# Interleaving small expert units with whole blocks: two units behind the last block, and the gate product ahead of the output product

## The chip, the cores and the metric

The kernel runs on one core of a Trainium2 chip. The metric is the time on the device of one execution, in microseconds (us), as the median of several executions. A core has a matrix engine (TensorE, PE in the profile, with its weight loads as PEld), VectorE (DVE), ScalarE (ACT), GpSimd (POOL, which here issues all gathers and scatters by index), SyncE (SP), and 16 DMA engines between device memory and the on-chip memories. Each engine works through its own list of instructions in the order in which the compiler put them; semaphores make an instruction wait for another engine or for a transfer.

## The reference

The reference is one transformer layer on x of shape 2 x 4096 x 512, all in float32: a layer norm with modulation, linear attention with 16 heads, a residual, a second layer norm, and a mixture of 8 experts of which each token takes 2. What matters here is the last part:

```python
gate_out = ragged_dot(sorted_xs, w_gate)              # per expert, 512 -> 2 x 512
activation = gelu(gate_out[:, 0, :]) * gate_out[:, 1, :]
expert_outputs = ragged_dot(activation, linear)       # per expert, 512 -> 512
out = einsum('blkd,blk->bld', out_by_token, combine_weights)
x = x + gb * out
```

There are 8192 tokens, so 16384 pairs of token and expert. How many fall on each expert is known only when the router has run.

## The kernel before, in words

The pairs of each expert are cut into units. A whole block has 512 tokens of one expert; there are always 25 of them (9 early, 16 late: `NEARLY`, `NLATE`). What is left over goes through small units of 128 tokens, of which 29 (`NSURE`) are always worked through and a few more behind a branch on the count.

**A whole block** (`block`, L1645) multiplies with seven products of half-size matrices in place of eight (`seven`, L1502): seven products for the first half of the gate weights, seven for the second, seven for the output weights, 21 in all. `gate_big` ends with gelu on ACT and with products and sums on DVE (L1611, L1612, L1620 to L1623) that make the left operands `aT` and `aS` of `linear_big`. The block is a generator: it yields between products, 22 times for one block (`STEPS`).

**A small unit** has four parts:

- `fetch_small` (L1675) gathers the gate weights of the unit's expert (`wgs`, 128 x 4096 float32, 2.1 MB, one buffer), the map of its tokens, and the token rows (`xg_s`).
- `turn_in` (L1685) transposes the rows on PE (`pxs`) and copies them with ACT.
- `gate_small` (L1696) first gathers the output weights (`wls`, 128 x 2048 float32, 1.05 MB, one buffer), then runs the two gate products (`pgs`, L1705) and makes the activation `ar` on ACT and DVE.
- `turn_out` (L1716) transposes `ar` (`pas`), and `linear_small` (L1726) runs the output product (`py`, L1731). `put` (L1461) scales the result on DVE (`y_s`, L1485) and adds it to the output rows with an indirect DMA (`out`, L1488). Each unit's additions wait for those of the unit before, since they may meet in the same row.

With one buffer each, the gather of the next `wgs` waits until the gate product that reads the old one is done on PE, and the gather of the next `wls` waits for the output product that reads the old one.

**The order of the work.** `smalls` (L1736) is a generator too, with two steps for each turn j: the first turns out unit j - 1 and turns in unit j, the second holds the products. One more turn than there are units empties the pipeline, so 29 units make 60 steps. `in_turn` (L1753) advances the blocks one step at a time and lets the small units follow in a fixed proportion; what has not been run when the count of block steps is reached runs after the loop:

```python
for n in range(1, count_one + 1):
    next(one, None)
    while done < count_other * n // count_one:
        next(other, None)
        done += 1
for g in (other, one):
    for _ in g:
        pass
```

So the order of the instructions on PE is nearly that of the program, with small differences where the compiler's scheduler places them. In the last stage of the kernel the 16 late blocks (352 steps) are mixed with the 29 small units (60 steps). Before the change the 60 steps are spread over the first 345 block steps, and the last 7 steps, the output products of the last block, run alone.

Of the kernel before, what the change touches and what calls it, by code (L numbers as in the profile page):

```python
# [33 lines left out]
NBIG = (NTOK * TOPK - E * (TB - 1) + TB - 1) // TB  # L34

NEARLY = (N * TOPK - E * (TB - 1) + TB - 1) // TB
NLATE = NBIG - NEARLY
# [8 lines left out]
NSURE = 29  # L46
# [7 lines left out]
def adaln_linear_attention_moe_kernel(  # L54
# [83 lines left out]
    def pool(stack, name, bufs=1, **kw):  # L138
        return stack.enter_context(
            tc.tile_pool(name=name, bufs=bufs, reuse_waits="tile", **kw)  # L140
        )
# [876 lines left out]
    count = {"cum": sm.tile([P, E], FP, tag="cum", name="cum")}  # L1018
# [401 lines left out]
    def gather(dst, src, ids):  # L1420
        return nc.gpsimd.indirect_dma_start(  # L1421
            out=dst, out_offset=None, in_=src, in_offset=IndirectOffsetOnAxis(ap=ids, axis=0)
        )

    def flat(t):
        return t.rearrange("p a k n -> p (a k n)")
# [8 lines left out]
    def fetch_map(ns, j, mrow, bufs):  # L1435

        mp = lists.tile([P, ns, 2], FP, tag=f"mp{ns}_{bufs}", name=f"mp_{ns}_{j}", bufs=bufs)
        got = gather(
            mp.rearrange("p t s -> p (t s)"),
            map_d.rearrange("(r t) s -> r (t s)", t=ns),  # L1440
            mrow,
        )
        for sent in scatters:
            manual_dep(got.ins, sent, "the map is whole")
        return mp
# [4 lines left out]
    def fetch_rows(where, ns, key, mp, bufs, src):  # L1450

        xg = []
        for t in range(ns):
            r = where.tile([P, C], FP, tag=f"xg{ns}", name=f"xg_{key}_{t}", bufs=bufs)
            gather(r, src, token(mp, t))
            xg.append(r)
        return xg
# [187 lines left out]
    def block(j):  # L1645

        more = j + 1 < NBIG

        soon = more and j + 1 != NEARLY
        if more:  # L1650
            fetch_big_rows(j + 1)
        yield from gate_big(j, 0)
        if more:
            fetch_gate(j + 1, 0)
        yield
        yield from gate_big(j, 1)
        if more:
            fetch_gate(j + 1, 1)
        if NEARLY <= j + 1 and j + 2 < NBIG:
            fetch_big_map(j + 2)  # L1660
        yield
        if soon:
            turn_big(j + 1)
        yield
        yield from linear_big(j)
        if more:
            fetch_lin(j + 1)
        if more and not soon:
            turn_big(j + 1)
        yield  # L1670
# [4 lines left out]
    def fetch_small(j):  # L1675
        wg = sw.tile([P, 2, 4, KH, QN], FP, tag="wgs", name=f"wgs_{j}", bufs=1)
        mrow, wrow = late["rows"]
        gather(wg.rearrange("p m q k n -> p (m q k n)"), wgate, wrow[:, j : j + 1])
        if (1, j) not in maps:
            maps[1, j] = fetch_map(1, j, mrow[:, j : j + 1], 4)  # L1680
        small[j] = [fetch_rows(sw, 1, f"s{j}", maps[1, j], 2, h2_d), wg]
        if j + 1 < NSURE:
            maps[1, j + 1] = fetch_map(1, j + 1, mrow[:, j + 1 : j + 2], 4)

    def turn_in(j):  # L1685
        xg = small[j].pop(0)[0]
        xT = sw.tile([P, KC, P], FP, tag="xTs", name=f"xTs_{j}", bufs=2)
        pt = psum["t"].tile([P, TB], FP, tag="tr", name=f"pxs_{j}")
        for k in range(KC):
            nc.tensor.transpose(  # L1690
                pt[:, k * P : (k + 1) * P], xg[:, k * P : (k + 1) * P], ident
            )
        nc.scalar.copy(xT.rearrange("p k n -> p (k n)"), pt)
        small[j].append(xT)

    def gate_small(j):  # L1696

        xT, wg = small[j].pop(), small[j].pop()
        wl = sw.tile([P, 4, KH, QN], FP, tag="wls", name=f"wls_{j}", bufs=1)
        gather(flat(wl), wlin, late["rows"][1][:, j : j + 1])  # L1700
        pg = []
        for half, quarters in enumerate(((0, 1), (3, 2))):
            p = psum["g"].tile([P, 2, QN], FP, tag="g", name=f"pgs_{j}_{half}")
            for k in range(KC):
                nc.tensor.matmul(  # L1705
                    p, xT[:, k, :], wg[:, :, quarters[k // KH], k % KH, :],
                    start=(k == 0), stop=(k == KC - 1),
                )
            pg.append(p.rearrange("p m n -> p (m n)"))
        ge = sw.tile([P, H], FP, tag="ges", name=f"ges_{j}", bufs=2)  # L1710
        nc.scalar.activation(ge, pg[0], AF.Gelu_apprx_tanh)
        ar = sw.tile([P, H], FP, tag="ar", name=f"ar_{j}", bufs=2)
        nc.vector.tensor_tensor(ar, pg[1], ge, ALU.mult)
        small[j] += [wl, ar]

    def turn_out(j):  # L1716

        ar = small[j].pop()
        pt = psum["t"].tile([P, TB], FP, tag="tr", name=f"pas_{j}")
        for hc in range(HC):  # L1720
            nc.tensor.transpose(pt[:, hc * P : (hc + 1) * P], ar[:, hc * P : (hc + 1) * P], ident)  # L1721
        aT = sw.tile([P, HC, P], FP, tag="aTs", name=f"aTs_{j}", bufs=2)
        nc.scalar.copy(aT.rearrange("p k n -> p (k n)"), pt)
        small[j].append(aT)

    def linear_small(j):  # L1726
        wl, aT = small.pop(j)
        p = psum["g"].tile([P, 2, QN], FP, tag="g", name=f"py_{j}")
        for hc in range(HC):
            q = (slice(0, 4, 3), slice(1, 3))[hc // KH]  # L1730
            nc.tensor.matmul(  # L1731
                p, aT[:, hc, :], wl[:, q, hc % KH, :], start=(hc == 0), stop=(hc == HC - 1)
            )
        put(f"s{j}", maps.pop((1, j)), [[p.rearrange("p h n -> p (h n)")]], False)

    def smalls(count):  # L1736


        for j in range(count + 1):
            if j:  # L1740
                turn_out(j - 1)
            if j < count:
                turn_in(j)
            yield
            if j:
                linear_small(j - 1)
            if j < count:
                gate_small(j)
                if j + 1 < count:
                    fetch_small(j + 1)  # L1750
            yield

    def in_turn(one, count_one, other, count_other):  # L1753

        done = 0
# [8 lines that stand above are left out]
# [35 lines left out]
    STEPS = 3 * 7 + 1  # L1799

    def blocks(j0, j1):
        for j in range(j0, j1):
            yield from block(j)
# [9 lines left out]
    for _ in block(NEARLY - 1):  # L1813
# [4 lines left out]
    psum.clear()  # L1818
    psum["t"] = pool(ctx, "ps_t3", 2, space=PSUM)
    psum["g"] = pool(ctx, "ps_g3", 6, space=PSUM)  # L1820
    in_turn(
        blocks(NEARLY, NBIG), STEPS * NLATE - STEPS // 3, smalls(NSURE), 2 * (NSURE + 1)
    )

    left = nc.values_load(late["left"], min_val=0, max_val=NSMALL)

# [62 lines left out]
```

## Time and profile before

| | us |
|---|---|
| median of 3 runs | 2370.75 |
| lowest, highest | 2366.18, 2374.37 |
| profiled execution, time | 2372.11 |
| profiled execution, span of the trace | 2370.4 |
| PE busy in the span | 2257.7 |
| last stage, where late blocks and small units are mixed | from about 1423 to the end |

The span is the time from the first to the last instruction in the trace; the execution's own time is 1.71 us longer. A line of a timeline gives the start, the busy time, the engine, the source line, the operation with the tiles that it writes and reads, and in brackets how long the engine had been idle before it and what ended that.

### The profile page before, as it was taken

What the parts mean: (1) busy time and instruction counts of PE and PEld (TensorE: products, weight loads), DVE (VectorE), ACT (ScalarE), POOL (GpSimd) and SP (SyncE); (2) the same over time, 40 slices, a digit from 0 to 9 for tenths busy, and PEclk for the clock granted to TensorE, in tenths of its full rate; (3) what the DMA queues carried; (4) which work ended last, traced back from release to release, by engine and by line L of the source; (5) the groups of instructions that cost most, each with busy time, mean ns of one, the idle gap of its engine ahead of it and who ended that gap; (6) DMA issues with size and microseconds to landing.
All of it is one profiled execution on the core that took longest, in us unless ns stands there. A gap on an engine that the chain in (4) does not pass through costs nothing. (4 is left out here: it accounts for less than half of the span.)

```text
span 2370.4 us, 26081 instructions
## 1 busy us (share of the span) xinstructions
PE 2257.7 (95%) x9456; PEld 1702.1 (72%) x9456; DVE 1523.0 (64%) x3251; ACT 535.0 (23%) x976; POOL 963.2 (41%) x840
## 2 busy tenths in 40 slices
PE   8999989999988999989998889999999999999997
PEld 4576657777766758878887767777777777777775
DVE  4866647786977756767876765555555555555554
ACT  1121212232323302333333411111111111111110
POOL 1266663003223242343535356444444444544432
PEclk9999999999999999999999989999999999999999
DMA  7688886444544444647684557777777777777774
GB/s 271 244 310 324 333 313 230 166 152 138 178 164 110 127 160 166 215 152 239 171 256 150 162 169 241 250 249 247 249 250 250 235 237 248 244 249 256 245 222 89
DMA packets 120189, 513.29 MB, mean 217 GB/s; under 512 B 19365, under 2 KB 22181, under 8 KB 84090
## 3 DMA queue, kind: packets, MB, share of 16 engines
q0 software_dynamic: 64704, 296.79, 40.1%
q1 hardware_dynamic: 41530, 164.45, 20.4%
q10 hardware_dynamic: 13824, 50.34, 5.5%
q8 instruction: 77, 1.26, 0.2%
q14 instruction: 54, 0.44, 0.1%
HBM read 378.97 MB, written 132.55 MB: 216 GB/s over the span
## 5 line engine op out<-in xcount | busy, mean ns | idle before, releaser
L1512 PE MATMUL p_g<-xT,wg 128*128 128x256 f32 x1600 | 373.0, 380 | 0.0
L1512 PEld LDWEIGHTS p_g<-xT,wg 128*128 128x128 f32 x1600 | 303.4, 191 | 45.7 <-issue 5.2
L1512 PE MATMUL p_g<-xS,wg 128*128 128x256 f32 x1200 | 286.6, 381 | 14.9 <-DVE quar_l L1520 7.6
L1512 PEld LDWEIGHTS p_g<-xS,wg 128*128 128x128 f32 x1200 | 227.4, 191 | 51.2 <-issue 8.1
L946 PE MATMUL po<-gm,qT 128*128 128x265 f32 (+1 forms) x1024 | 247.2, 391 | 4.6 <-issue 2.6
L795 PE MATMUL pa<-k,xh 128*128 128x512 f32 x512 | 234.2, 611 | 16.4 <-ACT k L774 16.3
L946 PEld LDWEIGHTS po<-gm,qT 128*128 128x128 f32 x1024 | 194.3, 194 | 40.2 <-issue 5.5
L1488 POOL DMA_INDIRECT out<-y_b,mp x100 | 162.7, 1627 | 129.2 <-DVE y_b L1485 101.2
L1153 POOL DMA_INDIRECT map_d<-pair,slot x128 | 133.5, 1043 | 176.0 <-DVE slot L1150 138.4
L1705 PE MATMUL pgs<-wgs,xTs 128*128 128x512 f32 x464 | 203.9, 592 | 0.0
L1512 PE MATMUL p_l<-wl,aT 128*128 128x256 f32 x800 | 193.7, 380 | 2.6 <-DVE part_l L1520 2.6
L795 PEld LDWEIGHTS pa<-k,xh 128*128 128x128 f32 x512 | 99.0, 196 | 134.4 <-issue 108.1
L617 POOL TENSOR_TENSOR wraw<-wraw 128x512 f32<-128x512 f32 x96 | 135.7, 1417 | 88.9 <-DMA wraw<-in_wgate 36.0
L1705 PEld LDWEIGHTS pgs<-wgs,xTs 128*128 128x128 f32 x464 | 88.2, 190 | 110.5 <-issue 109.5
L1512 PEld LDWEIGHTS p_l<-wl,aT 128*128 128x128 f32 x800 | 148.8, 191 | 23.6 <-DVE part_l L1520 3.0
L1512 PE MATMUL p_l<-wl,aS 128*128 128x256 f32 x600 | 144.0, 383 | 0.6 <-DVE aS L1622 0.6
L679 POOL TENSOR_TENSOR xs<-xT 128x512 f32<-128x512 f32 x16 | 21.3, 1330 | 292.1 <-DMA xT<-in_xturned 173.1
L1520 DVE TENSOR_TENSOR quar_g<-part_g,p_g 128x512 f32<-128x512 f32 x150 | 102.5, 684 | 51.1 <-PE p_g L1512 46.5
L1611 ACT ACTIVATE ge<-quar_g 128x512 f32<-128x512 f32 x100 | 63.0, 630 | 312.2 <-DVE quar_g L1520 300.9
L1512 PEld LDWEIGHTS p_l<-wl,aS 128*128 128x128 f32 x600 | 114.3, 192 | 17.9 <-issue 1.4
L1421 POOL DMA_INDIRECT xg_b<-h_d,mp x100 | 100.9, 1009 | 64.1 <-issue 32.5
L1520 DVE TENSOR_TENSOR part_g<-part_g,p_g 128x512 f32<-128x512 f32 x100 | 68.5, 686 | 83.8 <-PE p_g L1512 78.8
(343 smaller groups left out, 3734.7 us busy)
## 6 DMA issues: line engine op xcount, KB each, us to landing
xT<-in_xturned SPq DMA_DIRECT2D x16, 1024.0 KB
x<-in_x SPq DMA_DIRECT2D x16, 1024.0 KB
q_d<-q ACTq DMA_DIRECT2D x64, 256.0 KB
xb_d<-x SPq DMA_DIRECT2D x16, 1024.0 KB
qi<-q_d SPq DMA_DIRECT2D x64, 256.0 KB
wraw<-in_wgate SPq DMA_DIRECT2D x16, 1024.0 KB
wgsum_d<-wraw SPq DMA_DIRECT2D x16, 1024.0 KB
xb<-xb_d SPq DMA_DIRECT2D x16, 1024.0 KB
```

Of the source, the lines that this page charges most:

```text
L617: nc.gpsimd.tensor_tensor(to, one, two, op)
L679: nc.gpsimd.tensor_tensor(s7, x00, x10, ALU.subtract)
L795: nc.tensor.matmul(pa, xh[t][:, g * P : (g + 1) * P], ks[t], start=(t == 0), stop=(t == NT - 1),)
L946: nc.tensor.matmul(po[:, C // 2 - EX + c0 : C // 2 - EX + c1], qT[:, g * P : (g + 1) * P], gm[:, g, c0:c1], start=(g == 0), stop=(g == KC ...
L1153: ins = nc.gpsimd.indirect_dma_start(out=map_d, out_offset=IndirectOffsetOnAxis(ap=slot[:, k, t : t + 1], axis=0), in_=pair[:, k, t, :], i ...
L1421: return nc.gpsimd.indirect_dma_start(out=dst, out_offset=None, in_=src, in_offset=IndirectOffsetOnAxis(ap=ids, axis=0))
L1488: ins = nc.gpsimd.indirect_dma_start(out=out[0:N, :] if early else out, out_offset=IndirectOffsetOnAxis(ap=token(mp, t), axis=0), in_=y, i ...
L1512: nc.tensor.matmul(bank[:, c, :], left(s, c, k), rhs[:, k, :], start=(k == 0), stop=(k == KH - 1),)
L1520: nc.vector.tensor_tensor(r, one, two, ALU.add)
L1611: nc.scalar.activation(ge, g, AF.Gelu_apprx_tanh)
L1705: nc.tensor.matmul(p, xT[:, k, :], wg[:, :, quarters[k // KH], k % KH, :], start=(k == 0), stop=(k == KC - 1),)
```

## The change

Two things change. In `smalls`, the second step of a turn runs the gate product of unit j first and the output product of unit j - 1 behind it; the fetch for unit j + 1 comes last. In the call of `in_turn`, the count of block steps becomes 352, all of them, and the count of small steps that go with them becomes 56. The last four small steps then run after the loop: the turning of units 27 (out) and 28 (in), the gate product of 28 with the output product of 27, the turning out of 28, and the output product of 28. The 56th step, with the gate product of 27 and the output product of 26, falls on the 352nd block step and so comes behind the last block's products too.

```diff
@@ smalls(count)
             yield
+            if j < count:
+                gate_small(j)
             if j:
                 linear_small(j - 1)
-            if j < count:
-                gate_small(j)
-                if j + 1 < count:
-                    fetch_small(j + 1)
+            if j + 1 < count:
+                fetch_small(j + 1)
             yield
@@ the last stage
-    in_turn(
-        blocks(NEARLY, NBIG), STEPS * NLATE - STEPS // 3, smalls(NSURE), 2 * (NSURE + 1)
-    )
+    in_turn(blocks(NEARLY, NBIG), STEPS * NLATE, smalls(NSURE), 2 * (NSURE + 1) - 4)
```

## The prediction

> **What bounds the kernel now.** I read the page's totals first, then the chain that ended last, then the busy time of each engine by stretches of the last stage, since both edits act only there. The totals put PE far ahead:
>
> ```profile
> PE 2257.7 (95%) x9456; PEld 1702.1 (72%) x9456; DVE 1523.0 (64%) x3251; ACT 535.0 (23%) x976; POOL 963.2 (41%) x840
> ```
>
> The chain is made of PE matmuls from about 1410 us to 2344.5 us. The stretches show how tight that is. The columns are the stretch, its length, the busy time of PE, PEld, DVE, ACT and POOL, the granted clock, the DMA share and GB/s:
>
> ```profile
> 1427.00:2344.00 917.00, 917.00 (x3788) 677.43 (x3788) 498.57 (x826) 146.72 (x256) 420.39 (x368) 1.00 0.76 241
> 2357.00:2371.00 14.00, 0.00 (x0) 0.00 (x0) 2.24 (x5) 0.00 (x0) 5.79 (x4) 0.61 0.57 76
> ```
>
> In the mixed stage PE is busy 917.00 of 917.00 us. No wait there can be removed, and an edit that only reorders its work can win nothing there. What is open is the end: 14 us in which PE has nothing left. The timeline of the end, PE and then POOL, shows who fills it:
>
> ```profile
> 2340.89 3.60 PE L1731 MATMUL py<-wls,aTs 128*128 128x512 f32 x8
> ...
> 2354.68 1.89 PE L1512 MATMUL p_l<-wl,aT 128*128 128x256 f32 x8
> ...
> 2356.56 1.56 POOL L1488 DMA_INDIRECT out<-y_b,mp  x1 [9.02 <-DVE y_b L1485]
> 2358.43 1.56 POOL L1488 DMA_INDIRECT out<-y_b,mp  x1 [0.30 <-issue]
> 2360.29 1.55 POOL L1488 DMA_INDIRECT out<-y_b,mp  x1 [0.30 <-issue]
> 2362.15 1.56 POOL L1488 DMA_INDIRECT out<-y_b,mp  x1 [0.30 <-issue]
> ```
>
> A block product takes 1.73 us by starts (a row's duration overlaps the next by some 0.16), so PE ends at 2354.68 + 1.73 = 2356.41. Then come the last block's four scatter-adds, and from the issue of the last to the end of the span 2370.4 - 2362.15 = 8.25 us.
>
> **The change, part by part.** It adds and removes no matmul and no DMA. I sum it against the span of 2370.4 us.
>
> *The exchange inside the loop.* Before, `py` of unit j - 1 stood in front of `pgs` of unit j. Its operands come from the step before, several block products earlier, so it did not wait, and PE shows no idle time to recover. After it, `wgs` of the next unit is issued behind the gate product as before, in a spacing that grows from 11.5 to 12.6 block steps per unit. `wls` of unit j is now asked for before its one buffer is free: on POOL its gather waits 3.43 us more, for `py`, and the scatter of unit j - 1 and the next map are queued behind it. The next user is a unit later, some 30 us away (`pgs` starts at 2284.32 and 2316.32 in consecutive units), against a load of about 5 to 9 us. Cost nothing; the cover is the block products between two units, and where there are none, the loads show. The evictions `ar` and `y_s` on DVE follow in the new order with six PSUM banks in turn; DVE has 498.57 us of work in 917.
>
> *Work moved behind the last block.* In the built program PE now ends with gate 27, output 26, transposes of 27 and 28, gate 28, output 27, transposes of 28, output 28. By starts a gate pair takes 6.87 us (2316.32 to 2323.18), an output product 3.43 (2340.89 to 2344.32), four transposes 0.44 or 0.43: 6.87 + 3.43 + 0.87 + 6.87 + 3.43 + 0.43 + 3.43 = 25.33 us. So the last block's products end 25.33 us earlier, at 2331.08.
>
> *A cover that goes.* The last block's second output product needs `aS`. After the last gate product (end 2339.16 + 1.73 = 2340.89) DVE needed until 2343.22 + 0.68 = 2343.90, 3.0 us, for it; `py` of 3.43 us hid that. Now the first output product (1.73) and eight transposes (0.87) lie there, 2.6 us: a stall of 0.4. Call T0 = 2331.5 the end of the last block on PE, and count from it.
>
> *Gate weights of unit 28, exposed.* Their one buffer is free when gate 27 ends, at T0 + 6.87. On POOL the gather stands behind the four scatter-adds of the last block, which today end 2363.71 - 2356.41 = 7.3 us after the block's last product. So it is issued at 7.6. How long 2.1 MB take behind such scatters, the trace shows at 2315.59, where two gathers of 1.05 MB follow four of them:
>
> ```profile
> 2313.72 1.56 POOL L1488 DMA_INDIRECT out<-y_b,mp  x1 [0.30 <-issue]
> 2315.59 1.00 POOL L1421 DMA_INDIRECT wl<-wlsum_d,wrowl  x1 [0.30 <-issue]
> 2316.89 0.98 POOL L1421 DMA_INDIRECT wls<-in_wlin,wrows  x1 [0.30 <-issue]
> ...
> 2323.00:2324.00 1.00, 1.00 (x5) 0.74 (x4) 0.54 (x1) 0.00 (x0) 1.00 (x1) 1.00 0.72 303
> 2324.00:2325.00 1.00, 1.00 (x6) 0.87 (x6) 0.15 (x1) 0.00 (x0) 0.33 (x1) 1.00 0.42 86
> ```
>
> The DMA drains at about 2324.1, 8.5 us after the first issue. The other end is the `wgs` gather at 2231.52 on a quiet DMA, whose bytes are through by about 2238.8, 7.3 us. I take 8.5, the row with the scatters: landed at 16.1 (14.9 to 16.7). PE has run out at 6.87 + 3.43 + 0.87 = 11.2 and idles 4.9 us.
>
> *The clock.* The same stage's start shows what PE does after such a gap:
>
> ```profile
> 1405.79 1.32 PE L1579 MATMUL px<-ident,xg_b 128*128 128x128 f32 x4 [4.86 <-DMA xg_b<-h_d,mp]
> ...
> 1409.73 3.62 PE L1512 MATMUL p_l<-wl,aS 128*128 128x256 f32 x8
> 1413.14 2.60 PE L1512 MATMUL p_l<-wl,aT 128*128 128x256 f32 x8
> 1415.58 1.67 PE L1512 MATMUL p_l<-wl,aS 128*128 128x256 f32 x7
> ```
>
> After 4.86 us of idling two products took 1415.58 - 1409.73 = 5.85 us where 3.45 is normal, 2.4 us lost; the granted clock was 0.50 in those slices. At 82.46, after 2.66 us of idling, the clock fell to 0.50 for about 3.4 us, 1.7 us lost. I take 2.0 per gap, between the two rows; the ends are 0 and 2.4. Gate 28 ends at 16.1 + 6.87 + 2.0 = 25.0, output 27 at 28.4; its weights, issued at about 10.6, landed long before.
>
> The Trainium skill speaks against this change here: "TensorE: Matmul & The Clock Gate", section "Part 1: The HAM clock gate", says that a window of about 3.4 us of idling halves the clock and that it takes about 3.4 us of steady work to undo it. By that rule a gap costs 1.7 us, and the sum below would be 0.6 us lower; the row at 1409.73 lost more, because the half clock lasted 4.8 us of dense work there.
>
> *Output weights of unit 28, exposed.* Their buffer is free when output 27 ends; POOL issues at 28.7. Scatters `y_s` of 27 and 28 are queued behind and are not ready earlier. Nearest row: the `wls` gather at 2222.59 on a quiet DMA with one scatter behind it, bytes through at about 2227.8, 5.2 us (bounds 4.7, and 7.2 from 2316.89 to 2324.1 behind another gather). Landed at 33.9; PE idles 5 us again. Output 28: 33.9 + 3.43 + 2.0 = 39.3.
>
> *The end.* DVE starts 0.2 us later, `y_s` takes 0.75, POOL issues 0.27 later: 40.6. The scatter of unit 27, issued near 30 and landing 5.28 us later (2345.57 to 2350.85 today), is no obstacle. With 8.25 us behind the last issue: T0 + 48.8 = 2380.3. Against 2370.4 that is +9.9 us. The profiled execution's time of 2372.11 lies 1.36 above the median of 2370.75, so I add the difference to the median: 2380.7.
>
> **The rivals.** *The gaps are short.* If both loads land at their lower bound (1.2 and 0.5 us sooner) and the clock stays up through both, 4.0 us go too: +4.2, 2375.0. For it: granting the clock seems not to follow the idle time exactly (2.66 us sufficed once). Against it: 4.86 us of idling did bring it down, and so did the end of PE's work, to 0.53 in the slice from 2360.
>
> *The loads come in time, and the end gets shorter.* The mechanism is the tail alone: one scatter-add at the end for four. If PE never waited for weights it would end at 2356.41 + 0.4, and 0.2 + 0.75 + 0.27 + 8.25 = 9.5 us later the span, at 2366.3: -4.1, 2366.6 as a median. It decides as soon as the two waits and their clock cost together fall under 4 us. One buffer each for `wgs` and `wls` and a gate product that ends only 3.43 + 0.87 us before its successor wants to start speak against it. Larger gains have no source, with PE at 917.00 of 917.00.
>
> *Worse transfers.* With 16.7 for the first load, 7.2 us for the second and 2.4 per clock gap: 0.6 + 2.0 + 0.8 more, +13.3, 2384.0. A stall in the mixed stage from the new phase of the two loops would come on top, a few us at most.
>
> **How the numbers follow.** About 0.3%, 7.1 us, is what a measurement of this kernel can tell from no change. The forecast (+7.1 to +12) has 0.55, worse transfers 0.17, short gaps 0.19, the shorter end 0.07, a gain that I can't place 0.02. Parts of the short gaps reach over the bound and parts of the forecast under it: slower 0.70, same 0.26, faster 0.04. The range runs from 2372.5, inside the short gaps, to 2389, where the worse transfers and a few us of stalls in the mixed stage end.
>
> **What would show it.** In the profile after: PE full from 1427 to about 2331; one gap of about 5 us in front of the last `pgs` group, ended by the DMA of `wgs`, one of about 5 us in front of the last `py`, ended by `wls`; the clock at 0.5 behind each; the last scatter one `y_s`, some 8 us ahead of the end. I am wrong if a gap is under 3 us, if the clock stays up, or if PE shows idle time in the mixed stage.

## The result and the profile after

| | kernel before | changed kernel |
|---|---|---|
| median, first set of runs (6 and 6) | 2368.16 | 2386.42 |
| changed over before, first set | | 1.0071 [1.0054, 1.0089] |
| changed over before, second set (runs of e0 below) | | 1.0057 [1.0038, 1.0075] |
| span of the profiled execution | 2370.4 | 2375.5 |

Times in us, intervals at 95%. The change costs 0.6 to 0.7%, some 13 to 17 us; +9.9 us was forecast, with a range up to 2389.

The two spans differ by only 5.1 us, because the executions differ before the change begins: the same code, up to the start of the mixed stage, took 8.6 us less in the profiled execution of the changed kernel, and in the later sets, measured on the chips that the record numbers 0, 9 and 13 (it names none for the first set), the kernel before takes about 2300 to 2308 us. So I set a mark in every trace, the short wait of PE at the first late block, and count from there:

```profile
1426.79 1.99 PE L1512 MATMUL p_g<-xS,wg 128*128 128x256 f32 x8 [1.11 <-DVE xS L1588]
```

That is the kernel before; in the changed kernel the same row reads

```profile
1418.20 1.99 PE L1512 MATMUL p_g<-xS,wg 128*128 128x256 f32 x8 [1.11 <-DVE xS L1588]
```

From the mark to the end of the span the kernel before takes 2370.4 - 1426.79 = 943.6 us, the changed kernel 2375.5 - 1418.20 = 957.3: 13.7 us more.

The mixed stage of the changed kernel, in the columns of the prediction, and its end:

```profile
1419.00:2323.00 904.00, 903.65 (x3774) 676.17 (x3773) 501.14 (x828) 144.30 (x252) 419.79 (x363) 1.00 0.75 239
2357.00:2376.00 19.00, 5.25 (x8) 2.08 (x8) 0.75 (x1) 0.00 (x0) 2.85 (x2) 0.70 0.36 85
```

PE is full again but for 0.35 us. That is the predicted cover in front of `aS`, in the last block, where `py` no longer stands:

```profile
2312.65 1.96 PE L1512 MATMUL p_l<-wl,aS 128*128 128x256 f32 x8 [0.35 <-PE pxs L1690]
```

Everything else lies behind the last block. The timeline of PE from there to its last work, and that of POOL from the load of the last gate weights on (the four scatter-adds of the last block are issued just ahead of it, from 2323.22 on):

```profile
2323.08 7.03 PE L1705 MATMUL pgs<-wgs,xTs 128*128 128x512 f32 x16
2329.95 3.60 PE L1731 MATMUL py<-wls,aTs 128*128 128x512 f32 x8
2333.38 0.60 PE L1721 MATMUL pas<-ident,ar 128*128 128x128 f32 x4
2333.82 0.60 PE L1690 MATMUL pxs<-ident,xg_s 128*128 128x128 f32 x4
2341.58 10.13 PE L1705 MATMUL pgs<-wgs,xTs 128*128 128x512 f32 x16 [7.16 <-DMA wgs<-in_wgate,wrows]
2351.55 3.60 PE L1731 MATMUL py<-wls,aTs 128*128 128x512 f32 x8
2354.99 0.60 PE L1721 MATMUL pas<-ident,ar 128*128 128x128 f32 x4
2361.56 5.25 PE L1731 MATMUL py<-wls,aTs 128*128 128x512 f32 x8 [5.97 <-DMA wls<-in_wlin,wrows]
```

```profile
2330.89 0.99 POOL L1421 DMA_INDIRECT wgs<-in_wgate,wrows  x1 [0.30 <-issue]
2333.82 0.97 POOL L1421 DMA_INDIRECT wls<-in_wlin,wrows  x1 [1.94 <-PE py L1731]
2335.20 1.61 POOL L1488 DMA_INDIRECT out<-y_s,mp  x1 [0.41 <-issue]
2355.42 0.96 POOL L1421 DMA_INDIRECT wls<-in_wlin,wrows  x1 [18.61 <-PE py L1731]
...
2367.88 1.58 POOL L1488 DMA_INDIRECT out<-y_s,mp  x1 [9.61 <-DVEq L1835]
```

The two gaps in brackets are the two exposed loads. The gate product behind the first gap takes 10.13 us where 7.03 is normal, the output product behind the second 5.25 where 3.60 is. The slices of one us show the clock behind the first gap (third number from the right):

```profile
2346.00:2347.00 1.00, 1.00 (x3) 0.48 (x2) 0.00 (x0) 0.00 (x0) 0.00 (x0) 0.50 0.00 0
2347.00:2348.00 1.00, 1.00 (x3) 0.36 (x2) 0.00 (x0) 0.00 (x0) 0.00 (x0) 0.66 0.00 0
2348.00:2349.00 1.00, 1.00 (x4) 0.40 (x3) 0.00 (x0) 0.60 (x1) 0.00 (x0) 1.00 0.00 0
```

### The profile page after: what moved, and what is told of

The parts are those of the page before. It is cut to its first block, busy times and chain, and to the rows that moved or that the text cites. A ratio compares the mean times of both kernels' runs of the same rounds, so it can differ in the third digit from the quotient of the medians.

```text
span 2375.5 us, 26094 instructions
## 1 busy us (share of the span) xinstructions
PE 2263.0 (95%) x9456; PEld 1705.7 (72%) x9456; DVE 1526.8 (64%) x3251; ACT 534.5 (22%) x976; POOL 963.1 (41%) x840
```

## Experiments

Two theories stood at the start. A: the whole cost lies behind the last block, in two waits for weights and the half clock behind each. B: the new order also slows the loop itself. "Mark to end" is counted as above; the kernel before has 943.6, the changed kernel 957.3. Ratios are to the kernel before, run beside.

| run | mark to end, us | ratio, interval |
|---|---|---|
| e0, the changed kernel again | 2319.1 - 1360.92 = 958.2 | 1.0057 [1.0038, 1.0075] |
| e1, order only | 2306.2 - 1362.23 = 944.0 | 0.9999 [0.9986, 1.0011] |
| e2, counts only | 2308.9 - 1356.66 = 952.2 | 1.0026 [1.0012, 1.0040] |
| e3, two buffers for `wls` | 2313.5 - 1362.33 = 951.2 | 1.0032 [1.0018, 1.0046] |
| e4, no `wgs` load for unit 28 | 2311.4 - 1362.26 = 949.1 | 1.0023 [1.0010, 1.0035] |
| e7, PE kept busy in the first gap | 2310.4 - 1354.64 = 955.8 | 1.0052 [1.0033, 1.0070] |
| e8, no `wls` load for unit 27 | 2313.3 - 1354.68 = 958.6 | 1.0070 [1.0052, 1.0087] |
| e9, fetch two units ahead | 2299.1 - 1357.17 = 941.9 | 0.9994 [0.9984, 1.0005] |
| e10, e8 without the scatter of unit 26 | 2318.8 - 1360.10 = 958.7 | a single execution |
| e11, no scatters of the last block | 2313.6 - 1358.67 = 954.9 | a single execution |

**e0: the changed kernel again.** No edit.

> The changed kernel itself, unaltered, for its size and for a second trace. Theory A (the whole cost lies behind the last block: two weight loads that PE waits for, and the half clock behind each): from the first full block of the mixed stage to the end of the span the trace takes 957 us again (before: 943.6), PE idles about 7 and 6 us in front of the last gate product and the last output product, and the median lies 12 to 19 us over the kernel before, the rest over 13.7 us being spread of the stages that the change doesn't touch. Theory B (the new order inside the loop also slows the mixed stage): PE shows idle time between 1430 and 2320 us, several us in sum.

958.2 from the mark, within 1 us of the first trace. The first gap and the request that it waits for:

```profile
2273.61 0.99 POOL L1421 DMA_INDIRECT wgs<-in_wgate,wrows  x1 [0.30 <-issue]
2285.47 9.93 PE L1705 MATMUL pgs<-wgs,xTs 128*128 128x512 f32 x16 [8.33 <-DMA wgs<-in_wgate,wrows]
```

The second gap is 5.94 us, and PE is busy 903.65 of 904.00 us of the mixed stage (1361 to 2265). Theory B finds nothing. The ratio, 13.1 us at this chip's 2308, agrees with the trace's 14.6; the 16.8 us of the first set has its lower bound at 12.8, so no further cost is needed to explain it.

**e1: the order alone.**

```diff
@@ smalls, in the kernel before
+            if j < count:
+                gate_small(j)
             if j:
                 linear_small(j - 1)
-            if j < count:
-                gate_small(j)
-                if j + 1 < count:
-                    fetch_small(j + 1)
+            if j + 1 < count:
+                fetch_small(j + 1)
```

> Only the order inside the small units' loop is changed (gate product ahead of the output product); the counts stay at 345 block steps and 60 small steps, so nothing moves behind the last block. Theory A: no change, -2 to +2 us, PE full in the mixed stage. Theory B: 3 us or more slower, with idle time of PE in the mixed stage.

No change, and PE without a gap, from the mixed stage to the last product:

```profile
1363.00:2291.00 928.00, 928.00 (x3839) 686.92 (x3837) 505.30 (x836) 147.36 (x257) 424.04 (x369) 1.00 0.75 239
```

B is refuted. Inside the loop the order costs nothing and gains nothing, since block products lie on both sides of it.

**e2: the counts alone.** The call of the changed kernel, with the old order in `smalls`.

> Only the counts are changed (352 and 56); the output product stays ahead of the gate product. Theory A: the order decides how much of the loads is exposed. With the old order the output weights of the last unit can be asked for before its gate product and arrive under it, so the last gap goes, while the weights of the unit before it and the gate weights of the last unit leave gaps of some 3 and 2 to 5 us: 3 to 9 us over the kernel before, and 5 to 10 us under the changed kernel. Theory B: as long as or longer than the changed kernel less a few us, with the mixed stage as in the kernel before.

By the traces 8.6 us more than the kernel before (943.6) and 8.2 more than e1 (944.0), 6.0 us more by the ratio. Five waits stand behind the last block, two of them for weights; the other three, 0.73 to 0.85 us each, are for the activation's way through ACT and DVE. The two and the last of the three:

```profile
2278.11 5.52 PE L1731 MATMUL py<-wls,aTs 128*128 128x512 f32 x8 [4.16 <-DMA wls<-in_wlin,wrows]
2287.15 7.10 PE L1705 MATMUL pgs<-wgs,xTs 128*128 128x512 f32 x16 [3.53 <-DMA wgs<-in_wgate,wrows]
...
2296.50 3.70 PE L1731 MATMUL py<-wls,aTs 128*128 128x512 f32 x8 [0.73 <-ACT aTs L1723]
```

The last output product waits only for the activation, as its weights came in under the gate product in front of it. So the counts alone make the change slower, and the order, free inside the loop, costs another 6 us where no block product is left: in the new order the request for the last output weights waits for the output product behind the gate product, and so comes after everything else.

**e3: two buffers for the output weights.**

```diff
-        wl = sw.tile([P, 4, KH, QN], FP, tag="wls", name=f"wls_{j}", bufs=1)
+        wl = sw.tile([P, 4, KH, QN], FP, tag="wls", name=f"wls_{j}", bufs=2)
```

> The changed kernel with two buffers in place of one for the small units' output weights. The last unit's output weights then needn't wait for the output product before it. Theory A: the gap of 6 us in front of the last output product goes, with about 1.6 us of half clock; some 1 us is left for the activation's way through VectorE and ScalarE. 5 to 8 us less than the changed kernel. The first gap stays within 2 us of 7.2. If the last scatter or its wait on the scatter before it ended the kernel, it would be less than 3 us.

7.0 us less than e0 by the traces: the second gap is 0.73 us, the last output product takes 3.70, and the first gap stays at 8.15.

```profile
2300.56 3.70 PE L1731 MATMUL py<-wls,aTs 128*128 128x512 f32 x8 [0.73 <-ACT aTs L1723]
```

**e4: no load of the last gate weights.** Unit 28 uses the tile of unit 27.

```diff
+        if j == NSURE - 1:
+            wg = late["wg"]
+        else:
...
+        late["wg"] = wg
```

> The changed kernel without the gather of the last small unit's gate weights: unit 28 computes with the weights of unit 27 (its rows of the output come from the wrong expert). Theory A (cost = two waits for weights plus the half clock behind them): the first gap of 7 to 8 us and the 3 us of half clock in the gate product go, less the 1 us that the copy of the turned rows needs: 9 to 10 us less than the changed kernel, so 3 to 6 us over the kernel before, with the second gap of 6 us left. Rival (the first gap would only be replaced by a wait for the scatters or for the activation): 3 us less or under.

9.1 us less than e0, 5.3 us over the kernel before by the ratio. In front of the gate product 0.73 us are left, for the copy of the turned rows, and it takes 7.13:

```profile
2279.21 7.13 PE L1709 MATMUL pgs<-wgs,xTs 128*128 128x512 f32 x16 [0.73 <-ACT xTs L1697]
```

The second gap is 6.04 us. e3 and e4 together take 16.1 us away, a little more than the 14.6 that the change costs in e0's trace.

**e7: PE kept busy in the first gap.**

```diff
+        if j == NSURE - 1:
+            warm = psum["t"].tile([P, TB], FP, tag="tr", name="warm")
+            for n in range(WARM):     # 7
+                nc.tensor.matmul(warm, ident, gb[:, 0], start=(n == 0), stop=(n == WARM - 1))
...      # one column of warm is copied away
```

> The changed kernel with seven idle products of 512 columns (identity by a constant tile, their result is used by nothing) on PE in the first gap, some 6 us of work in a gap of 7 to 8. Theory A's clock term: the granted clock stays at 1.0 through the last gate product, which takes 6.9 us in place of 9.9, so the end comes 2 to 3 us earlier, while the wait for the weights ends at the same time. If the slow gate product were due to something other than the granted clock (weights still arriving, say), it stays near 9.9 us and nothing is gained.

```profile
2271.12 6.28 PE L1703 MATMUL warm<-gb,ident 128*128 128x512 f32 x14 [0.24 <-ACT aTs L1730]
2278.89 7.11 PE L1712 MATMUL pgs<-wgs,xTs 128*128 128x512 f32 x16 [1.49 <-DMA wgs<-in_wgate,wrows]
```

The load lands as late as before, 11.55 us after its issue, and the gate product runs in 7.11 us in place of 9.93 in e0. So the slow product was the clock. The end comes 2.4 us earlier than in e0 by the traces; the ratios can't tell the two apart.

**e8: no load of the output weights of unit 27.** My sum had called that load, issued 2.9 us behind the gate weights, harmless.

```diff
+        if j == NSURE - 2:
+            wl = late["wl"]
+        else:
...
+        late["wl"] = wl
```

> The changed kernel without the gather of the output weights of unit 27, which is issued 2.9 us behind that of the gate weights of unit 28 (unit 27 computes with the output weights of unit 26). Theory C (the first gap is 2.3 us longer than predicted since that transfer of 1.05 MB, which the prediction took to be harmless, shares the DMA engines with the 2.1 MB that PE waits for): from issue to landing the gate weights take 8.3 to 9.5 us in place of 10.7 to 11.9, and the first gap is 5 to 6 us. Rival (the scatters ahead of it set the landing): 10.5 us or more, as before.

A miss: 2278.92 - 2267.35 = 11.57 us from issue to PE's start. The theory called C falls; sharing with that load is not why the first gap is longer than predicted.

**e10: the scatter behind it left out too.**

```diff
@@ put, on top of e8
+            if key == f"s{NSURE - 3}":
+                continue
```

> The kernel without the output weights of unit 27, now also without the scatter-add of unit 26 (its rows are not added to the output), so that nothing is issued behind the gather of the last gate weights while it runs. Theory D (a scatter-add keeps the DMA engines busy for some 2 us per 128 rows, as at the end of the kernel before, where four of them hold the DMA share near 1 for 8 us; the scatters ahead of the gather and the one behind it share the engines with it): from issue to landing 9.0 to 10 us in place of 11.6, the gap in front of the last gate product 6 to 7 us. Rival (only what is ahead of the gather counts, or the gather alone is slow): 11 us or more.

A miss for theory D as it stands, since it has what comes behind the gather share the blame: PE starts at 2284.30, 11.5 us after the issue at 2272.79, as the rival has it. Yet with nothing behind it nearly all bytes are through at about 2281.2, 8.4 us after the issue, near the 8.5 of the sum. The slices (last two columns: DMA share, GB/s) show why:

```profile
2280.00:2281.00 1.00, 0.00 (x0) 0.00 (x0) 0.00 (x0) 0.00 (x0) 0.00 (x0) 0.50 0.70 295
2281.00:2282.00 1.00, 0.00 (x0) 0.00 (x0) 0.00 (x0) 0.00 (x0) 0.00 (x0) 0.50 0.16 66
2282.00:2283.00 1.00, 0.00 (x0) 0.00 (x0) 0.00 (x0) 0.00 (x0) 0.00 (x0) 0.50 0.04 16
2283.00:2284.00 1.00, 0.00 (x0) 0.00 (x0) 0.00 (x0) 0.00 (x0) 0.00 (x0) 0.50 0.04 16
```

From 2282 on one 16 KB packet per us is left, at a share of 0.04, which is 0.6 of one engine's time in 16 x 1 us. The trace also records when each of the 16 DMA engines reports its part of a transfer. Here 14 reports come between 2280.61 and 2281.86, one at 2282.66 and the last at 2284.16, 0.14 us before PE starts: one engine works off its last rows while the others are done. The tile is complete with the slowest engine. The Trainium skill says the same of such transfers: by "DMA: Bandwidth & Descriptors", section "Why a DMA increments its semaphore by 16 and not by 1", all 16 engines must report before a gather issued by GpSimd counts as landed.

**e11: no scatters of the last block.**

```diff
@@ put, in the changed kernel
+            if key == f"b{NBIG - 1}":
+                continue
```

> The changed kernel without the four scatter-adds of the last block (its rows are not added to the output). The gather of the last gate weights is then issued when the gate product before it ends, 0.3 to 0.5 us earlier, and finds the DMA engines idle. Theory D: 6.5 to 9 us from issue to landing in place of 10.7 to 11.9, the first gap 3 to 5 us in place of 7 to 8. Rival (a gather of 2.1 MB in rows of 16 KB takes 10 us by itself): 10 us or more, and the gap keeps its size.

```profile
2270.87 0.96 POOL L1421 DMA_INDIRECT wgs<-in_wgate,wrows  x1 [24.04 <-PE pgs L1707]
2279.24 9.38 PE L1707 MATMUL pgs<-wgs,xTs 128*128 128x512 f32 x16 [4.33 <-DMA wgs<-in_wgate,wrows]
```

2279.24 - 2270.87 = 8.37 us from issue to start, and the first gap is 4.33 us in place of 8.33, although the load of `wls` for unit 27 and the scatter of unit 26 ran with it. So the four scatter-adds ahead cost the load 2.3 us (against the changed kernel) to 3.5 us (against e0), and the gap 2.8 to 4.0 (half a us of the gap's part is that the request goes out sooner). The reports of the engines show where the time goes. The first engine is done with the gather 7.4 us after the issue in e11, 7.8 in e10, 8.5 in the changed kernel and 8.7 in e0; the last one after 8.2, 11.4, 10.6 and 11.7. So the scatters hold up the slowest engine most. Why some engines lag so far was not tried further.

**e9: a version with the loads ahead.** Two buffers each for `wgs` and `wls`, the fetch two units ahead, one buffer for `ges` and `ar` to make room.

```diff
-            if j + 1 < count:
-                fetch_small(j + 1)
+            if j + 2 < count:
+                fetch_small(j + 2)
...      # the counts of buffers, and a fetch of unit 1 ahead of the loop
```

> The changed order and counts with two buffers for the small units' gate and output weights and the fetch two units ahead, so that both loads are under way before the last block ends (the activation's tiles have one buffer each, for room). Theory A: no gap over 1.5 us behind the last block, the clock stays up; behind the last block come 27 us of PE work with two short waits for the activation, and one scatter ends the kernel: 1 to 4 us under the kernel before, 15 to 18 us under the changed kernel. Rival (a chain of scatters, each waiting for the one before, ends the kernel): 0 to 4 us over the kernel before.

Behind the last block PE waits 0.73 us before the gate product and 0.68 before the output product, and the clock stays up. From the mark it is 1.7 us under the kernel before and 16.3 under e0; the ratio of 0.9994 can't tell it from the kernel before. Its last scatter waits for the one of unit 27 to land, so the rival's chain of scatters does end this kernel, but at a small price: the result is ready at 2290.29, and the scatter goes out at 2291.47. No version tried beats the kernel before by a measurable margin.

## Why the prediction was right, and which terms were off

The direction and the mechanism came out as forecast: PE stays full in the mixed stage (0.35 us of 904 idle), the two gaps stand in front of the last `pgs` and the last `py`, each ended by the DMA named, the clock stands at 0.50 behind both, and a single `y_s` scatter ends the kernel. Of the rivals, the short gaps and the shorter end are refuted by the traces of the changed kernel; e9 reaches the shorter end with another buffer for both weights; by its trace it is then worth 1.7 us, where 4.1 was worked out, and the ratio can't tell that from nothing. "Worse transfers", at +13.3, came nearest by the number, but not by its terms: the first load landed at 18.5 and 19.7 us (the two traces of the table below) where it had 16.7, the second took 6.1 where it had 7.2, and the two clock terms were 3.1 and 1.6 where it had 2.4 each.

The size was too small by 4 to 5 us in the traces, and the cost lies above the +7.1 to +12 that got a chance of 0.55. The measured median of 2386.42 is even above the 2384.0 of "worse transfers"; the range takes it in only because its upper end allowed for a few us of stalls in the mixed stage, which no trace shows. That much was luck. The sum, term by term, counted from the end of the last block on PE (2323.08 after; 904.9 us behind the mark, where the sum had 904.7):

| term | predicted | changed kernel | e0 |
|---|---|---|---|
| issue of the last gate weights, from the last block's end | 7.6 | 7.8 | 7.8 |
| their landing, from issue | 8.5 | 10.7 | 11.9 |
| half clock in the gate product | 2.0 | 3.1 | 2.9 |
| last `wls`, from the end of the output product to its issue | 0.3 | 0.4 | 0.4 |
| its landing, from issue | 5.2 | 6.1 | 6.1 |
| half clock in the output product | 2.0 | 1.6 | 1.6 |
| from the last scatter's issue to the end | 8.25 | 7.6 | 7.6 |
| end, from the last block's end | 48.8 | 52.4 | 53.3 |

The term furthest off is the landing of the gate weights: its upper bound of 9.1 us (16.7 less 7.6) was exceeded in every trace in which the last block's scatters ran ahead of it, 10.7 to 11.9 us. It was read from the row at 2315.59 as the time at which most bytes were through, not the time at which a waiting PE would be let go; in e10 these two are 3 us apart. The trace of the kernel before had the later time too: the last row of those two gathers ended at 2325.20 and the last engine reported at 2325.59, 10.0 us after the issue in place of 8.5. The same reading put the `wgs` gather at 2231.52 at 7.3 us, though its last row ended at 2239.93, 8.4 us after the issue, near the 8.37 of e11. And it put the `wls` gather at 2222.59 at 5.2 us, though its last engine reported at 2228.64, 6.05 us after the issue; that is the 0.9 us by which the second landing was short. What is left of the first landing, 0.7 to 1.9 us over 10.0, stays open: the row had four scatters ahead too, spread over 9.2 us from the first issue to the last end, here 7.4, but no run varies that spacing.

The clock term was the other one. With 4.4 to 6.1 us of dense work at half clock in the traces the loss behind the first gap is 2.2 to 3.1 us, and that behind the second runs from 1.6 to 3.0 us in the traces with a second gap. The upper end of 2.4 was too low. The 1.7 us per gap that the prediction worked out from the rule of the Trainium skill's "TensorE: Matmul & The Clock Gate", section "Part 1: The HAM clock gate", would have been lower still in nearly all of them; the measurement decides.

The remark that the output weights of unit 27 "landed long before" was right for what it was meant, since their product did not wait, and e8 shows that their sharing the DMA is not what moved the first gap.

## What to carry to other kernels

Work that is moved behind the last covering loop is costed by its own loads: with one buffer per weight tile, a load can start only when the product before it has ended, and once the block products are gone the whole load is idle time, plus the restart of the clock. An order that is free inside such a loop (e1) can cost several us at its end (e2 against e0), so both are to be tested apart. Read a load's time from the issue to the start of whoever waits for it, or to the last engine's report where nobody waits, not to the point where the bytes per us fall off.

## What had not been expected of the hardware

- Four scatter-adds of 128 rows of 2 KB, issued within 7.4 us, delay a 2.1 MB gather behind them by 2.3 to 3.5 us (8.4 us in e11, 10.7 in the changed kernel, 11.9 in e0). The first of the 16 DMA engines to be done is 0.4 to 1.3 us later by them, the last 2.3 to 3.5: in e10 a single engine ends 1.5 us after the one before it and 2.3 after the other 14, and in the changed kernel four engines end together, 0.7 us after the rest.
- The half clock lasted from 2341.58 to about 2347.7 in the changed kernel, 6.1 us of dense work, longer than in either row of the kernel before (4.8 and 3.4 us).
- The length of a gap alone did not tell whether the clock falls. In e2 PE idled for 3.53 us in front of the last gate product, the granted clock stayed at 1.00, and the product took 7.10 us; in the kernel before the clock fell after 2.66 us of idling, at 82.46.
